# An attention layer and a non-local layer on one core: the first image's x kept whole, projections gathered in one gap, first-block differences made early, and one eviction per block moved to ScalarE

## The chip, the cores and the metric

The kernel runs on one core of one Trainium2 chip. The metric is device time in microseconds (us), from the first to the last instruction of the core and a little around it; lower is better. Engines are called PE (TensorE), DVE (VectorE), ACT (ScalarE), POOL (GpSimd) and SP (SyncE, which here only starts DMAs).

## What is computed

Two layers run one after the other on an image batch x of shape (2, 256, 64, 64), all in float32. With n = 64 * 64 = 4096 positions, 8 heads and d = 32:

```python
qkv = einsum('oc,bchw->bohw', w_qkv, x)                  # q, k, v
scores = einsum('bhdi,bhdj->bhij', q, k) / sqrt(d)       # 4096 x 4096 for each head
out = einsum('bhij,bhdj->bhdi', softmax(scores), v)
x = einsum('oc,bchw->bohw', w_proj, out) + x
# second layer: a non-local block with pooled keys, a 1x1 convolution, batch norm and a residual
```

The scores aren't stored: the kernel finds the maximum of every row of scores in a pass of its own, and uses it in a second pass over the same products.

## The kernel before, in words

A "quad" is four heads of one image; there are four quads, numbered n = 0 to 3, two for each image. A quad's attention is cut into eight blocks (i = 0 to 7) of 512 queries, and a block into 32 steps (j = 0 to 31) of 128 keys: 1024 steps in all. The order of the work is written out by hand, as generators that the main loop advances (`attend`, L551 to L591); each engine executes its own list of instructions in order. The list is nearly the order of the code; now and then the build moves a single instruction a little ahead. One such place matters here: `neg` of the next block (L380) stands ahead of DVE's add of step 26 (L473), though the code issues it after that add.

One step of block (n, i) holds, on PE: four score matmuls (`score`, L439, in two pairs, written into two PSUM tiles `s` that are kept over the whole block, each step adding the difference between its keys and those of the step before); four matmuls of the maxima pass of the *next* block (`product`, L286); and four matmuls of the step before that apply the weights to v (`weigh`, L463, tile `w`). ACT takes the exponential of both score tiles (L574, 128 x 1024 each). POOL adds up half of the exponentials for the softmax's denominator (L491, one 128 x 1024 add for each step), and starts an accumulating DMA for the other half in every second step (L497). DVE adds `w` to the running numerator `blk.num`, a slice of the result's tile y (L473).

The maxima pass of block (n, i + 1) runs through `maxes` while block (n, i) is worked on, two products in each half step, and is four steps ahead (`LEAD = 4`). Heads 0 and 1 take the plain way: DVE reduces each product of 512 keys (L298). Heads 2 and 3 take pairs of key chunks (`pair`, L300 to L308): the maximum of a and b is a + relu(b - a), so one product uses a difference of keys (`kd` or `last_kd`), ACT takes its relu into a tile `over` (L305), and DVE adds it to the second product and takes the maximum in one instruction (L312). A pair costs DVE one pass for 1024 keys where the plain way costs two. At the first block of quads 1 to 3 only the first half of the keys goes in pairs (L352), because `last_kd` still holds the differences of the quad before. Head 3 begins and ends each block with a plain product, so at the change of block, in step 27, DVE has one plain reduction more, and then the reduction `neg` (L380). POOL turns `neg` into three bf16 rows (L141 to L145), and PE and ACT into the tile `rows` (`make_rows`, L150 and L158, in step 30).

[...] four in the two score tiles, and four in the pool `ps_m` (`scratch`, L71), which gives its banks out in turn to the maxima products, to `w`, to the projections, to `rows` and to the denominator. A matmul into a bank waits until the bank's last reader is done.

The projections that make q, k and v for later blocks ("items", `make`, L168) are put between steps: `during` (L267) lists three for each block, and the loop issues them at j = 11, 19 and 27 (L588). For i below 6 they are q of the block after next, then k and v of the next quad; for i = 6 they are k, k, q, for i = 7 v, v, q. An item waits for its piece of x, loaded by SP into the only buffer of the pool `xs` (L171). For the last quad only the q items are left. `renew` (L250) has POOL make the key differences of the next quad at the end of block 7 and at the start of the next block.

A block's denominator is made in the next block: in its step 5 POOL makes `whole` (L510), in step 8 PE adds up the partitions (`den`, L518), and in step 27 POOL scales the numerator (L549).

Before the first block there is a start phase (L803 to L817): the items of quad 0, in the order k, q, k, v, q, v and then k, k, v, v, each cut in two halves with one group of four maxima products between halves.

Of the kernel before, what the change touches and what calls it, by code (L numbers as in the profile page):

```python
# [9 lines left out]
F32 = mybir.dt.float32  # L10
# [6 lines left out]
N = HH * WW  # L17
# [5 lines left out]
P = 128  # L23
NC = C // P
NB = 512
NI = N // NB
NJ = N // P
# [8 lines left out]
def conv_attention(  # L36
# [13 lines left out]
    nc = tc.nc  # L50
# [25 lines left out]
    def single(name):  # L76
        return probs.tile([P, 2, NB], F32, tag="one", name=name, bufs=ONES)
# [9 lines left out]
    def load_x(b, i, t):  # L87
        nc.sync.dma_start(
            out=t, in_=x[b].rearrange("(o p) n -> p o n", p=P)[:, :, bass.ts(i, NB)]
        )  # L90
        return t
# [76 lines left out]
    def make(what, n, i):  # L168
        b, qd = QUAD[n]
        if (b, i) not in held:  # L170
            name = f"x_{what}_{n}_{i}"  # L171
            if attending:
                held.clear()
                to = xs.tile([P, NC, NB], F32, tag="x", name=name)
            else:
                to = single(name)
            held[b, i] = load_x(b, i, to)
        xc = held[b, i]
        name = f"{what}_{b}_{qd}_{i}"
        pq = scratch(name)  # L180
        if what == "v":
            if i == 0:
                v[n] = qkv.tile([P, NJ, QH, D], F32, tag="v", name=f"v_{n}")
            for j in range(NB // P):
                for c in range(NC):
                    nc.tensor.matmul(  # L186
                        pq[:, bass.ts(j, P)],
                        xc[:, c, bass.ts(j, P)],
                        wv_sb[:, c, bass.ts(qd, P)],
                        start=(c == 0),  # L190
                        stop=(c == NC - 1),
                    )
                if j % 2 == 1:
                    yield
            nc.scalar.copy(v[n][:, bass.ts(i, NB // P)].rearrange("p j h d -> p (j h d)"), pq)
            return
        for c in range(NC):
            nc.tensor.matmul(  # L198
                pq,
                wqk_sb[:, c, qd, 0 if what == "q" else 1, :],  # L200
                xc[:, c, :],
                start=(c == 0),
                stop=(c == NC - 1),
            )
            yield
        if what == "q":
            to = q[n, i] = qkv.tile([P, NB], F32, tag="q", name=f"q_{n}_{i}", bufs=3)
        else:
            if i == 0:
                k[n] = qkv.tile([P, N], F32, tag="k", name=f"k_{n}")  # L210
            to = k[n][:, bass.ts(i, NB)]
        nc.scalar.copy(to, pq)
        if what == "k" and i % 2 == 0 and i > 0 and n == 0:
            between(n, i // 2 - 1)
        if what == "k" and i == NI - 1 and n == 0:
            rounds(n)
        if what == "k" and i % 2 == 1 and n == 0:
            if i == 1:
                kd[n] = qkv.tile([P, NI // 4, NB], F32, tag="kd", name=f"kd_{n}")
            differences(n, i // 2, (kd[n] if i < NI // 2 else last_kd)[:, i // 2 % (NI // 4), :])  # L220
        elif what == "k" and i == NI // 2 - 1:
            kd[n] = qkv.tile([P, NI // 4, NB], F32, tag="kd", name=f"kd_{n}")
            for c in range(2):
                differences(n, c, kd[n][:, c, :])
# [5 lines left out]
    def differences(n, c, to):  # L230
        two = k[n][:, bass.ts(c, 2 * NB)]
        nc.gpsimd.tensor_sub(to, two[:, NB:], two[:, :NB])  # L232
# [31 lines left out]

    def during(n, i):  # L267
        if i < NI - 2:
            return [("q", n, i + 2), ("k", n + 1, i), ("v", n + 1, i)]
        if i == NI - 2:  # L270
            return [("k", n + 1, i), ("k", n + 1, i + 1), ("q", n + 1, 0)]
        return [("v", n + 1, i - 1), ("v", n + 1, i), ("q", n + 1, 1)]


    reduced, cut = None, None
# [7 lines left out]
    def product(n, i, g, h, keys, ps=None):  # L283
        if ps is None:
            ps = scratch(f"ps_{n}_{i}_{g}_{h}")
        nc.tensor.matmul(  # L286
            ps,
            q[n, i][bass.ts(h, D), bass.ts(g, P)],
            keys[bass.ts(h, D), :],
            start=True,  # L290
            stop=True,
        )
        return ps
# [6 lines left out]
    def pair(n, i, g, h, jp):  # L300

        nonlocal cut
        ps = product(n, i, g, h, (kd[n] if jp < NI // 4 else last_kd)[:, jp % (NI // 4), :])
        over = work.tile([P, NB], F32, tag="over", name=f"over_{n}_{i}_{g}_{h}")
        cut = nc.scalar.activation(over, ps, AF.Relu)  # L305
        yield
        joint(product(n, i, g, h, k[n][:, bass.ts(2 * jp, NB)]), over, g, h, jp)
        yield  # L308
# [39 lines left out]
    def of_head(n, i, h):  # L348

        chunks = 0 if h < 2 else NI // 2 if i == 0 and n > 0 else NI  # L352
        pairs = [(g, jp) for jp in range(chunks // 2) for g in range(G)]
        plains = [(g, j) for g in range(G) for j in range(chunks, NI)]
        if h == 3:
            if not plains:
                g, jp = pairs.pop()
                plains = [(g, 2 * jp), (g, 2 * jp + 1)]
            plain(n, i, plains[0][0], h, plains[0][1])
            plains = plains[1:]  # L360
            yield
        for x in pairs:
            yield from pair(n, i, x[0], h, x[1])
        for x in plains:
            plain(n, i, x[0], h, x[1])
            yield

    def maxima(n, i):
        if (n, i) == (0, 0):
            yield from first_block()  # L370
        else:
            heads = [of_head(n, i, h) for h in range(QH)]
            for step in range(G * NI):

                for two in (0, 1), ((2, 3) if step % 2 == 0 else (3, 2)):
                    for h in two:
                        next(heads[h])
                    yield
        neg = work.tile([P, NB // P, QH], F32, tag="neg", name=f"neg_{n}_{i}")
        nc.vector.tensor_reduce(neg, part, AX.X, ALU.max, negate=True)  # L380
        rows.append(negate(f"{n}_{i}", neg))
        if i == 0 and n > 0:
            nc.vector.memset(part[:, :, 2:, :], LEAST)


    rows = []
# [8 lines left out]
    def advance(steps, n=1):  # L395
        for _ in range(n):
            next(steps, None)
# [3 lines left out]
    def make_rows():  # L401

        for i, r in enumerate(rows):
            if callable(r):
                if i in seen:
                    rows[i] = r()
                seen.add(i)


    def attend(b, y):  # L410
# [48 lines left out]
        def weigh(blk, j, p):  # L459

            w = scratch(f"w_{blk.name}_{j}")
            for h in range(QH):
                nc.tensor.matmul(  # L463
                    w[bass.ts(h, D), :],
                    v[blk.n][:, keys(j), h, :],
                    p[h // 2][:, h % 2, :],
                    start=True,
                    stop=True,
                )
            if j == 0:  # L470
                nc.vector.tensor_copy(blk.num, w)
            else:
                nc.vector.tensor_add(blk.num, blk.num, w)  # L473

# [77 lines left out]
        for qd in range(QUADS):  # L552
            for i in range(NI):
                blk = Block(qd, i)
                items = [x for x in during(blk.n, i) if x[1] < len(QUAD)]
                both = [None, None]
                for j in range(NJ):
                    if j % 2 == 0:
# [24 lines left out]
                    if j % 2 == 0:  # L583
                        make_rows()
                        if i > 0 and blk.n + 1 < len(QUAD) or i == 0 and blk.n > 0:
                            with tc.issue_after(added.ins) if added else ExitStack():
                                renew(i, j, blk.n)
                    elif j % 8 == 3 and j > 8 and items:  # L588
                        advance(make(*items.pop(0)), 9)
        weigh(*waiting)  # L590
        return normalize(blk)  # L591

# [204 lines left out]

    LEAD = 4
    AFTER = 8
    attending = False  # L800


    items = [("k", 0), ("q", 0), ("k", 1), ("v", 0), ("q", 1), ("v", 1)]  # L803
    for i in range(2, NI, 2):
        items += [("k", i), ("k", i + 1), ("v", i), ("v", i + 1)]
    for n, (what, i) in enumerate(items):
        pieces = make(what, 0, i)
        for piece in range(3):
            advance(pieces)
            if n > 3 and piece < 2:  # L810
                advance(maxes)
    advance(maxes, 4)
    advance(maxes)
    make_rows()
    advance(maxes, LEAD - 1)
    make_rows()
    advance(maxes, LEAD)  # L817
    held.clear()
    attending = True
    for b in range(B):  # L820
        y = big.tile([P, NC, N], F32, tag="y", name=f"y{b}")
        normal = attend(b, y)
# [57 lines left out]
```

## Time and profile before

| what | us |
|---|---|
| median of 3 runs | 3923.11 |
| the 3 runs | 3920.67 to 3923.43 |
| profiled execution, its own time | 3922.51 |
| its span, first to last instruction | 3920.7 |
| first weigh matmul of block (0, 0) | 105.98 |
| weigh matmuls of the first step, block (0, 2) to block (0, 3) | 308.82 to 410.68 |
| the same, block (3, 2) to block (3, 3) | 3054.85 to 3153.74 |

| engine | busy us | share of the span |
|---|---|---|
| PE | 3882.0 | 99% |
| DVE | 2940.4 | 75% |
| ACT | 2654.9 | 68% |
| POOL | 3051.9 | 78% |

A group line of the profile names the source line, the engine, the operation, the tile written and the tiles read, then shapes and count, then busy time in us, the mean in ns, and the idle time of the engine just before these instructions with what ended it. A line of the timeline has the start in us from the span's beginning, the length in us, the engine, the line, the operation and tiles, the count of instructions merged, and in brackets the idle time before. PE's matmuls are pipelined, so overlapping lengths are no contradiction, and its 99% isn't a measure of how well it is used: within a step PE often sits between the stages of a chain. A float32 matmul stands in the trace as two instructions.

### The profile page before, as it was taken

The numbers are of one execution on the slowest core, as the hardware profiler recorded it, in microseconds if no ns is written. First come the engines' busy times: TensorE is split into PE (matmuls) and PEld (weight loads), VectorE is DVE, ScalarE is ACT, GpSimd is POOL, SyncE is SP. The second block draws the span as 40 slices with busy tenths as digits, with TensorE's granted clock in tenths as the row PEclk, the third lists the DMA queues.
The fourth block names the chain that finished last, engine by engine and source line by source line (L and its number), as shares of the span: only waits on it lengthen the run. The fifth ranks groups of instructions, "written<-read, shape, count | busy, mean of one in ns | idle before, by whom it ended". The sixth has DMA issues, their size and how long they took to land.

```text
span 3920.7 us, 69957 instructions
## 1 busy us (share of the span) xinstructions
PE 3882.0 (99%) x27452; PEld 1370.0 (35%) x27452; DVE 2940.4 (75%) x5483; ACT 2654.9 (68%) x3296; POOL 3051.9 (78%) x1926
## 2 busy tenths in 40 slices
PE   8999999999999999999999999999999999999998
PEld 3333333333333333343333333333433333332333
DVE  5888888888888888874458888888888888885444
ACT  4777777777777777741137777777677787787011
POOL 1788888889888888871448889898899999997043
PEclk9999999999999999999999999999999999999999
DMA  1688888887888888880018888888888888889100
GB/s 57 139 168 169 167 170 168 174 169 167 166 167 169 165 169 169 172 195 6 22 38 167 167 173 170 170 171 175 165 173 169 169 170 168 167 167 188 54 16 27
DMA packets 113931, 569.40 MB, mean 145 GB/s; under 512 B 20296, under 2 KB 22600, under 8 KB 52416
## 3 DMA queue, kind: packets, MB, share of 16 engines
q0 software_dynamic: 68832, 501.25, 63.7%
q1 hardware_dynamic: 44080, 62.88, 4.6%
q8 instruction: 215, 3.52, 0.4%
q14 instruction: 116, 0.95, 0.1%
q10 hardware_dynamic: 688, 0.79, 0.1%
HBM read 54.78 MB, written 8.88 MB: 16 GB/s over the span
## 4 chain that ended last, share of the span: by engine, by line
PE 53%; DVE 2%; DMA 1%; ACT 0%; issue 0%; POOL 0%; DVEq 0%; ACTq 0%; POOLq 0%
PE s L439 14%; PE w L463 13%; PE ps L286 11%; PE y L736 6%; PE g L661 1%; DVE r L750 1%; PE f L704 1%; PE proj L604 1%; PE f L770 1%; PE q L198 1%; PE den L518 1%; PE tp L645 0%; PE tp L641 0%; PE v L186 0%; PE k L198 0%; DMA x_res<-in_x_dram 0%
## 5 line engine op out<-in xcount | busy, mean ns | idle before, releaser
L491 POOL TENSOR_TENSOR p<-p,p 128x1024 f32<-128x1024 f32 x945 | 2350.5, 2487 | 363.4 <-ACT p L574 338.4
L574 ACT ACTIVATE p<-s 128x1024 f32<-128x1024 f32 x2048 | 2085.9, 1023 | 593.3 <-PE ps L286 528.5
L286 PE MATMUL ps<-k,q 32*128 32x512 f32 x6232 | 2016.1, 627 | 4.0 <-DVE part L298 1.7
L298 DVE TENSOR_REDUCE part<-ps 128x1 f32<-128x512 f32 x2136 | 1369.0, 685 | 541.8 <-PE ps L286 541.6
L463 PE MATMUL w<-p,v 128*32 128x512 f32 x8192 | 1091.9, 605 | 0.6 <-ACT p L574 0.6
L439 PE MATMUL s<-q,mid_kd 32*128 32x512 f32 x3072 | 767.4, 615 | 0.0
L473 DVE TENSOR_TENSOR y<-y,w 128x512 f32<-128x512 f32 x992 | 679.1, 685 | 47.1 <-PE w L463 46.4
L312 DVE CUSTOM_DVE_ANT_0 ps<-ps,over 128x512 f32<-128x512 f32 x980 | 674.5, 691 | 34.3 <-PE ps L286 31.2
L286 PEld LDWEIGHTS ps<-k,q 32*128 32x128 f32 x6232 | 628.1, 183 | 43.3 <-DVE part L298 8.9
L305 ACT ACTIVATE over<-ps 128x512 f32<-128x512 f32 x916 | 541.9, 592 | 18.0 <-PE ps L286 12.6
L286 PE MATMUL ps<-kd,q 32*128 32x512 f32 x1056 | 517.0, 594 | 0.7 <-POOL kd L232 0.7
L439 PE MATMUL s<-q,kd 32*128 32x512 f32 x2048 | 512.2, 615 | 0.4 <-ACT p L574 0.3
L439 PE MATMUL s<-q,last_kd 32*128 32x512 f32 x2048 | 509.8, 614 | 0.7 <-ACT p L574 0.7
L463 PEld LDWEIGHTS w<-p,v 128*32 128x32 f32 x8192 | 161.1, 108 | 804.6 <-DVE part L298 775.0
L286 PE MATMUL ps<-last_kd,q 32*128 32x512 f32 x904 | 438.0, 593 | 2.4 <-POOL last_kd L232 2.4
L439 PEld LDWEIGHTS s<-q,mid_kd 32*128 32x128 f32 x3072 | 262.0, 183 | 413.9 <-ACT over L305 225.6
L497 POOL DMA_DIRECT2D p<-p x448 | 392.2, 875 | 4.4 <-issue 3.1
L439 PEld LDWEIGHTS s<-q,kd 32*128 32x128 f32 x2048 | 177.1, 183 | 295.4 <-ACT over L305 171.9
L439 PEld LDWEIGHTS s<-q,last_kd 32*128 32x128 f32 x2048 | 176.7, 183 | 275.8 <-ACT over L305 162.7
L736 PE MATMUL y<-p,kv 128*128 128x512 f32 x512 | 240.0, 608 | 6.4 <-DVE r L750 6.4
L785 ACT ACTIVATE p<-f 128x1024 f32<-128x1024 f32 x64 | 65.5, 1024 | 248.5 <-PE f L770 219.2
L732 POOL TENSOR_TENSOR sums<-sums,p 128x512 f32<-128x512 f32 x96 | 121.3, 1264 | 113.7 <-ACT p L785 109.9
(113 smaller groups left out, 2686.7 us busy)
## 6 DMA issues: line engine op xcount, KB each, us to landing
p<-p POOLq DMA_DIRECT2D x478, 1024.0 KB, 7.5
x_k<-in_x_dram SPq DMA_DIRECT2D x32, 512.0 KB
x_q<-in_x_dram SPq DMA_DIRECT2D x30, 512.0 KB
x_res<-in_x_dram SPq DMA_DIRECT2D x16, 512.0 KB
out_dram<-z SPq DMA_DIRECT2D x16, 512.0 KB
r<-flat SPq DMA_DIRECT2D x120, 64.0 KB
x_v<-in_x_dram SPq DMA_DIRECT2D x6, 512.0 KB
wqk_sb<-in_wqk_dram ACTq DMA_DIRECT2D x1, 512.0 KB
```

The costliest lines, as they stand in the source:

```text
L286: nc.tensor.matmul(ps, q[n, i][bass.ts(h, D), bass.ts(g, P)], keys[bass.ts(h, D), :], start=True, stop=True,)
L298: reduced = nc.vector.tensor_reduce(part[:, g, h, j : j + 1], ps, AX.X, ALU.max)
L305: cut = nc.scalar.activation(over, ps, AF.Relu)
L312: reduced = nc.vector.tensor_tensor_reduce(out=ps, in0=ps, in1=over, scale=1.0, scalar=LEAST, op0=ALU.add, op1=ALU.max, accum_out=part[:, ...
L439: nc.tensor.matmul(s[:, t, :], kj[bass.ts(h, D), :], q[blk.n, blk.i][bass.ts(h, D), :], start=False, stop=True, skip_group_check=j > 0,)
L463: nc.tensor.matmul(w[bass.ts(h, D), :], v[blk.n][:, keys(j), h, :], p[h // 2][:, h % 2, :], start=True, stop=True,)
L473: nc.vector.tensor_add(blk.num, blk.num, w)
L491: added = nc.gpsimd.tensor_add(blk.sums[0], blk.sums[0], p[0])
L497: sent = nc.gpsimd.dma_start(out=blk.sums[n], in_=two, accum_op=ALU.add)
L574: nc.scalar.activation(p[pair], s, AF.Exp, scale=scale)
L732: nc.gpsimd.tensor_add(acc[i][NC], acc[i][NC], p[:, j, :])
L736: nc.tensor.matmul(acc[i][o], wg[:, 2 * t + j, bass.ts(o, P)], p[:, j, :], **edge)
```

## The change

It has six parts.

1. The first image's x is loaded whole, by eight DMAs at the very start, into the space of the result's tile y (`x0`). The start phase no longer loads x into `single` buffers.
2. The start phase has a new order. k 0, k 1 and q 0 come first. Then come k 2 to k 7, v 0 and v 1, each an undivided item followed by four groups of maxima products; then q 1, and v 2 to v 7 with half a step of the next maxima pass before each.
3. Items. For i below 6, q stays at j = 11; k and v of the next quad share one load of x and come together at j = 30, in the gap in which `make_rows` also works. Block 6 holds five items (k and v at 11, q at 19, k and v at 30), block 7 one (q at 7). Blocks of the last quad have only their q item, as before.
4. `before_all`: at step 8 of block 7, POOL makes the last two differences of the next quad's keys into `first_kd`, in the buffer where x was. So heads 2 and 3 go in pairs over all keys in the first block of every quad, and the clearing of `part` (L383) goes away.
5. In step j = 26 of every block but the very last, `w` isn't added by DVE from PSUM: ACT copies it to a tile `t` in SBUF (a buffer of the tag `over`), and DVE adds `t` to `blk.num`. In the built program the ACT copy stands right after the exponential of step 27, and the DVE add stands where the old add stood, right behind `neg`.
6. Loop bookkeeping: `during` returns a dictionary by step.

```diff
@@ make
-            if attending:
-                held.clear()
-                to = xs.tile([P, NC, NB], F32, tag="x", name=name)
-            else:
-                to = single(name)
-            held[b, i] = load_x(b, i, to)
+            held.clear()
+            held[b, i] = load_x(b, i, xs.tile([P, NC, NB], F32, tag="x", name=name))
@@ during
+    first_kd = {}
+
     def during(n, i):
         if i < NI - 2:
-            return [("q", n, i + 2), ("k", n + 1, i), ("v", n + 1, i)]
+            return {11: [("q", n, i + 2)], NJ - 2: [("k", n + 1, i), ("v", n + 1, i)]}
         if i == NI - 2:
-            return [("k", n + 1, i), ("k", n + 1, i + 1), ("q", n + 1, 0)]
-        return [("v", n + 1, i - 1), ("v", n + 1, i), ("q", n + 1, 1)]
+            return {
+                11: [("k", n + 1, i), ("v", n + 1, i)],
+                19: [("q", n + 1, 0)],
+                NJ - 2: [("k", n + 1, i + 1), ("v", n + 1, i + 1)],
+            }
+        return {7: [("q", n + 1, 1)]}
+
+    def before_all(n):
+        held.clear()
+        first_kd[n] = xs.tile([P, NI // 4, NB], F32, tag="x", name=f"first_kd_{n}")
+        for c in range(2):
+            differences(n, NI // 4 + c, first_kd[n][:, c, :])
@@ pair
-        ps = product(n, i, g, h, (kd[n] if jp < NI // 4 else last_kd)[:, jp % (NI // 4), :])
+        those = kd[n] if jp < NI // 4 else first_kd[n] if i == 0 and n > 0 else last_kd
+        ps = product(n, i, g, h, those[:, jp % (NI // 4), :])
@@ of_head
-        chunks = 0 if h < 2 else NI // 2 if i == 0 and n > 0 else NI
+        chunks = 0 if h < 2 else NI
@@ maxima
-        if i == 0 and n > 0:
-            nc.vector.memset(part[:, :, 2:, :], LEAST)
@@ weigh
             if j == 0:
                 nc.vector.tensor_copy(blk.num, w)
+            elif j == NJ - LEAD - 2 and (blk.n, blk.i) != (len(QUAD) - 1, NI - 1):
+                t = work.tile([P, NB], F32, tag="over", name=f"w_{blk.name}")
+                nc.scalar.copy(t, w)
+                nc.vector.tensor_add(blk.num, blk.num, t)
             else:
                 nc.vector.tensor_add(blk.num, blk.num, w)
@@ attend
-                items = [x for x in during(blk.n, i) if x[1] < len(QUAD)]
+                items = during(blk.n, i)
...
-                    elif j % 8 == 3 and j > 8 and items:
-                        advance(make(*items.pop(0)), 9)
+                        if (i, j) == (NI - 1, 8) and blk.n + 1 < len(QUAD):
+                            with tc.issue_after(added.ins):
+                                before_all(blk.n + 1)
+                    for item in items.get(j, ()):
+                        if item[1] < len(QUAD):
+                            advance(make(*item), 9)
@@ the start phase
-    attending = False
-    items = [("k", 0), ("q", 0), ("k", 1), ("v", 0), ("q", 1), ("v", 1)]
-    for i in range(2, NI, 2):
-        items += [("k", i), ("k", i + 1), ("v", i), ("v", i + 1)]
-    for n, (what, i) in enumerate(items):
-        pieces = make(what, 0, i)
-        for piece in range(3):
-            advance(pieces)
-            if n > 3 and piece < 2:
-                advance(maxes)
-    advance(maxes, 4)
-    advance(maxes)
-    make_rows()
-    advance(maxes, LEAD - 1)
-    make_rows()
-    advance(maxes, LEAD)
+    x0 = big.tile([P, NC, N], F32, tag="y", name="x0")
+    for i in range(NI):
+        held[0, i] = load_x(0, i, x0[:, :, bass.ts(i, NB)])
+    for what, i in (("k", 0), ("k", 1), ("q", 0)):
+        advance(make(what, 0, i), 3)
+    for what, i in [("k", i) for i in range(2, NI)] + [("v", 0), ("v", 1)]:
+        advance(make(what, 0, i), 3)
+        advance(maxes, G)
+    advance(make("q", 0, 1), 3)
+    for i in range(2, NI):
+        advance(maxes)
+        advance(make("v", 0, i), 3)
+        if i in (3, 5):
+            make_rows()
+    advance(maxes, 2 * LEAD - NI + 2)
```

More of the change, by code (lines that the diff above doesn't have):

```diff
@@ L799, in conv_attention @@
     AFTER = 8
-    attending = False
-    items = [("k", 0), ("q", 0), ("k", 1), ("v", 0), ("q", 1), ("v", 1)]
-    for i in range(2, NI, 2):
-        items += [("k", i), ("k", i + 1), ("v", i), ("v", i + 1)]
-    for n, (what, i) in enumerate(items):
-        pieces = make(what, 0, i)
-        for piece in range(3):
-            advance(pieces)
-            if n > 3 and piece < 2:
-                advance(maxes)
-    advance(maxes, 4)
-    advance(maxes)
-    make_rows()
-    advance(maxes, LEAD - 1)
-    make_rows()
-    advance(maxes, LEAD)
+    x0 = big.tile([P, NC, N], F32, tag="y", name="x0")
[13 more added lines that the diff above has]
+    advance(maxes, 2 * LEAD - NI + 2)
     held.clear()
-    attending = True
     for b in range(B):
```

## The prediction

> **What bounds the kernel now.** I read the engines' shares first, then the chain of waits, then the timeline of one step and of the change of block.
>
> ```profile
> PE 3882.0 (99%) x27452; PEld 1370.0 (35%) x27452; DVE 2940.4 (75%) x5483; ACT 2654.9 (68%) x3296; POOL 3051.9 (78%) x1926
> ...
> L491 POOL TENSOR_TENSOR p<-p,p 128x1024 f32<-128x1024 f32 x945 | 2350.5, 2487 | 363.4 <-ACT p L574 338.4
> ...
> L473 DVE TENSOR_TENSOR y<-y,w 128x512 f32<-128x512 f32 x992 | 679.1, 685 | 47.1 <-PE w L463 46.4
> ```
>
> PE is the bound, but 99% overstates it: in a step its three groups stream 6 x 0.43 = 2.56 us, and a step lasts 2.96 us. The rest is a closed chain: w, then score and maxima products, then DVE's reduction of the first product, whose bank the next w needs. POOL's adds fill 2.49 us of a step, its DMA starts more: it is nearly always busy. The chain prices what lies between steps:
>
> ```profile
> 2066.70 1.92 PE q L198 x4
> ...
> 2117.87 1.98 PE v L186 x16
> ...
> 2168.55 1.91 PE q L198 x4
> ...
> 2888.57 1.91 PE q L198 x4
> 2987.46 1.91 PE q L198 x4
> ```
>
> q to q, a block with three items lasts 101.85 us, one of the last quad with only q 98.89. So k and v together cost 2.96 there, though k is 1.91 and v 1.98: about 0.94 of v is free. The timeline of block (3, 2) shows why:
>
> ```profile
> 3131.59 1.06 PE L463 MATMUL w<-p,v 128*32 128x512 f32 x8
> ...
> 3133.80 1.89 DVE L298 TENSOR_REDUCE part<-ps 128x1 f32<-128x512 f32 x3 [0.39 <-PE ps L286]
> 3134.55 1.06 PE L463 MATMUL w<-p,v 128*32 128x512 f32 x8
> ...
> 3135.61 0.69 DVE L312 CUSTOM_DVE_ANT_0 ps<-ps,over 128x512 f32<-128x512 f32 x1
> ...
> 3135.70 0.84 POOL L497 DMA_DIRECT2D p<-p  x1
> ...
> 3136.30 2.62 POOL L491 TENSOR_TENSOR p<-p,p 128x1024 f32<-128x1024 f32 x1
> ...
> 3136.46 0.29 DVE L380 TENSOR_REDUCE neg<-part 128x16 f32<-128x128 f32 x1
> ...
> 3136.66 0.68 DVE L473 TENSOR_TENSOR y<-y,w 128x512 f32<-128x512 f32 x1
> ...
> 3137.26 1.99 DVE L298 TENSOR_REDUCE part<-ps 128x1 f32<-128x512 f32 x3
> ...
> 3137.40 1.12 PE L286 MATMUL ps<-k,q 32*128 32x512 f32 x2
> ...
> 3138.45 1.06 PE L463 MATMUL w<-p,v 128*32 128x512 f32 x8
> ```
>
> w to w is 2.96 us, then 3.90 at the change of block. DVE has three reductions in a row, the joint pass, neg, and only then the add of w. A product waits for that add's bank until 3137.40, and w 26's successor comes 0.94 late. With a v item at this place, DVE's extra work lies beside PE's. Note POOL: its add is in flight from 3136.30 to 3138.92, over DVE's add.
>
> [...] (1) [...] Today's add reads w in PSUM, one SBUF input; the new one reads `blk.num` and `t`, two. The trace holds a case with two, L489 in the last block:
>
> ```profile
> L489 DVE TENSOR_TENSOR p<-p,p x15: 1218/1226/4104, 3551.1 to 3625.5; 128x1024 f32<-128x1024 f32 x15
> ```
>
> (count, then shortest/median/longest ns), and from the timeline there:
>
> ```profile
> 3556.53 2.00 DVE L489 TENSOR_TENSOR p<-p,p 128x1024 f32<-128x1024 f32 x1
> ...
> 3560.70 2.36 POOL L491 TENSOR_TENSOR p<-p,p 128x1024 f32<-128x1024 f32 x1
> ...
> 3562.59 1.56 DVE L489 TENSOR_TENSOR p<-p,p 128x1024 f32<-128x1024 f32 x1
> ```
>
> Alone it takes 1.22. At 3562.59 POOL's add still had 0.47 to run: it took 1.56, 0.34 more. At 3556.53, 0.91 left: 0.78 more. At 3551.11 it took 4.10, with POOL's add behind a DMA start at its side. So DVE waits for POOL's add to end, less 0.14. (2) [...] So what stands behind the held add waits too; the trace agrees, nothing starts behind L489 until it is done. [...]
>
> **The change, part by part.** Sums are against the profiled execution (3922.51, span 3920.7), 0.6 below the median of 3923.11.
>
> *Step 26 through ACT.* ACT is idle then (no relu in step 27), so its copy of 0.59 hides, and the bank comes free early: PE's wait at 3137.40 goes. What is late next is DVE. Its add is ready at 3136.66, behind neg as now; POOL's add has begun 0.36 earlier and holds until 3138.92. By (1) DVE waits to 3138.78, adds in 0.60 (the spacing of back-to-back passes), and the reduction that now starts at 3137.26 starts at 3139.38. It takes 0.69, and 0.06 later w 27 starts: 3140.13, in place of 3138.45. The change of block then costs 5.58 - 2.96 = 2.62 over a plain step, not 0.94. Queued behind the held add are the two reductions, the next plain one and the add of w 27; w 27 waits for the first. Bounds of the unknown stall: 0 (DVE first; then DVE's row of passes alone makes the step 3.48, an excess of 0.52) to 2.9 (as at 3551.11). I take 2.12, because the offset of 0.30 to 0.38 stands in 25 of the 31 changes of block that I compared, blocks without a k or v item among them.
>
> *Items, i below 6, quads 0 to 2: 18 blocks.* Now: k 1.92, v 1.98 with the change of block hidden in it, rows 0.34 (w to w at step 30): 4.24. Then: rows, k and v in one gap: 0.34 + 1.92 + 1.98 less one 0.2 turn-round of PE (between two projections it streams on: 1.71 for k) = 4.02. With 2.62 bare, 6.64: +2.40 each, **+43.2**. The item queue in SP: one load fewer, each with 13 to 19 steps of 2.96 us of cover; if that cover failed, a load's 7 us would show.
>
> *Blocks 6 and 7 of quads 0 to 2.* Now 102.49 + 106.58 (w to w): block 7 has DVE reductions beyond what a step holds (3.4 in every second step, +3.9 in all), and q items used in the very next step (+0.6 each). Then: 32 x 2.96 = 94.6, den 0.87, block start 0.17. Block 6: + 3.70 (k, v) + 1.92 (q) + 2.62 + 4.02 = 107.9. Block 7: + 1.92 + 2.62 + 0.34 = 100.5. Sum 208.4, -0.7 each, **-2**. Pairs cost ACT 16 more relus of 0.59 in a block, as in every other block: hidden. POOL's two `first_kd` passes (1.3 each) fill its spare 0.15 a step up to step 26; POOL's backlog in the next block, which now costs block (3, 0) some 1.5 us at `den`, would grow by 2 without the stall, but the stall gives POOL 2 back: **+1** (0 to +4).
>
> *Last quad, i = 0 to 5.* No items move; 2.62 for 0.94: +1.68 x 6 = **+10**. In (3, 6) no maxima pass follows, DVE has room: 0.
>
> *Start.* k 0, k 1, q 0 end at 13.5 (as k, q, k do now). Then eight times an item and two pairs. The joint passes between 80.4 and 89.3, without items, show 2.9 us a pair; with two half items now 4.26, so 1.4 of 1.8 is not hidden: 2 x 2.9 + 1.4 = 7.2, x 8 = 57.6, ending at 71.1. q 1 with its copy 2.6, six times half a step and v 3.0, rows and two half steps 1.5: 93.2, against 99.28 now for the first row subtraction, and half a us less to the first w: **-6.6** (-17 with items hidden, -1 with nothing hidden). The eight loads are issued at once and the last has 20 us.
>
> Sum: -6.6 + 43.2 - 2 + 1 + 10 = +45.6: 3968.1, on the median's scale 3968.7, some 3969.
>
> **The rivals.**
>
> [...] The margin is 0.36 us by start, less if POOL's add really begins when its DMA start ends (3136.54). If POOL waits 0.6 instead, the excess is 0.52: 2.1 less at 30 changes of block, -63, and POOL's backlog +3: 3909. For it: POOL did wait at 3580.97 (3.13 for 2.36), where DVE had begun 0.32 before. Against: at 3551.11 DVE lost though it had begun 0.36 before POOL. It decides from the point where DVE's add starts before POOL's.
>
> *The clock drops as well.* PE stands still from 3137.54 to 3140.13, 2.6 us. [...] Here matmuls took 1.06 to 1.22 instead of 0.59 from 92 to 102, after a gap of 1.69 us; after one of 1.98 (L604's wait for y) they did not. At half clock 2.56 of PE work takes 5.12; [...] half of the 30 cases +21, all +43: 3990 to 4012.
>
> *A short stall*, about a third of 2.1 with the start at its best: 3920, no change.
>
> **Chances.** 0.2% (7.8 us) is about what a measurement of this kernel can tell from no change. Stall as computed 0.48; with the clock 0.23; DVE first 0.24; short stall 0.05. Slower 0.71, same 0.05, faster 0.24. The forecast is the likeliest, 3969; its own range, from start and stall bounds, is 3950 to 3992. The range that holds 8 in 10 reaches into both rivals: 3906 to 4003.
>
> **What would show it.** In the profile after: DVE's add that reads `over` at 2.7 to 2.8 us mean (about 0.69 if DVE is first, with POOL adds of 3.1 beside it); w 26 to w 27 at 5.6 (3.5); k to v spaced 1.7 in the gap of step 30, and about 4.0 + 2.96 there; block 7 with no steps of 3.4; first w near 99. The forecast is wrong if the new add is short.

## The result, and the profile after

The changed kernel takes 4047.54 us (median of 5 runs, 4046.62 to 4050.64); the kernel before, run beside it, 3923.11. The ratio is 1.0322 with a 95% interval of 1.031 to 1.0334: slower, by 124 us. The prediction was 3969, with a range up to 4003: the sign was right, the size was not. The profiled execution took 4046.81, its span is 4045.0.

The engines' shares and three groups of the profile after:

```profile
PE 3916.0 (97%) x27452; PEld 1374.0 (34%) x27452; DVE 3003.2 (74%) x5480; ACT 2695.8 (67%) x3372; POOL 3070.0 (76%) x1932
...
L504 POOL TENSOR_TENSOR p<-p,p 128x1024 f32<-128x1024 f32 x945 | 2346.8, 2483 | 367.5 <-ACT p L587 355.7
...
L470 PE MATMUL w<-p,v 128*32 128x512 f32 x8192 | 1112.9, 616 | 91.5 <-DVE part L307 90.8
...
L486 DVE TENSOR_TENSOR y<-y,w 128x512 f32<-128x512 f32 x961 | 658.3, 685 | 75.3 <-PE w L470 74.2
```

PE is busy 34 us longer with the same 27452 matmuls, so some of them ran slower. POOL's adds (2487 ns before) and DVE's plain add of w (685) are what they were. But w, before which PE stood idle for 0.6 us in all, now waits 91 us for DVE's reduction of the first product, the step that closes the chain. The line before the change:

```profile
L463 PE MATMUL w<-p,v 128*32 128x512 f32 x8192 | 1091.9, 605 | 0.6 <-ACT p L574 0.6
```

The instructions of the new add's line (count, then shortest, median and longest in ns):

```profile
L484 DVE TENSOR_TENSOR y<-y,w x31: 681/4022/4103, 187.6 to 3654.9; 128x512 f32<-128x512 f32 x31
```

4.02 us in the median, where I had 2.72 (2.12 of wait and 0.60). The timeline of block (3, 2), the same place as shown before, shows what it waits for:

```profile
3238.43 1.07 PE L470 MATMUL w<-p,v 128*32 128x512 f32 x8
...
3239.57 0.58 ACT L483 COPY w<-w 128x512 f32<-128x512 f32 x1
...
3240.16 2.63 POOL L504 TENSOR_TENSOR p<-p,p 128x1024 f32<-128x1024 f32 x1
...
3240.55 4.02 DVE L484 TENSOR_TENSOR y<-y,w 128x512 f32<-128x512 f32 x1
...
3242.47 1.54 POOL L562 TENSOR_TENSOR y<-y,r 128x512 f32<-128x512 f32 x1
3243.67 0.99 POOL L141 CAST terms<-neg 128x16 bf16<-128x16 f32 x1
3244.49 1.87 DVE L307 TENSOR_REDUCE part<-ps 128x1 f32<-128x512 f32 x3
...
3245.22 1.66 PE L470 MATMUL w<-p,v 128*32 128x512 f32 x8 [3.62 <-DVE part L307]
```

The copy on ACT is in time, and `neg` is too. DVE's add starts 0.39 after POOL's add, as foreseen. But POOL has a second operation right behind: L562, the scaling of the numerator of the block before. DVE's add ends at 3244.57, 0.56 after that multiplication, not after the add of step 27. The reductions stand behind it, and w 27 (the weigh matmuls of step 27) starts 6.79 us after w 26, where the block before the change had 3.90. Then the clock of PE, which the trace records as the granted share of full speed: four stretches of 3.4 us from 3239.4 (columns: stretch, its length, busy time and instructions of PE, weight load, DVE, ACT and POOL, then the granted clock, the DMA share and GB/s):

```profile
3239.40:3242.80 3.40, 2.21 (x20) 1.29 (x16) 3.29 (x5) 2.89 (x5) 3.40 (x4) 1.00 0.69 142
3242.80:3246.20 3.40, 0.98 (x8) 0.16 (x8) 3.40 (x4) 0.40 (x1) 3.11 (x7) 0.91 0.93 193
3246.20:3249.60 3.40, 3.40 (x20) 1.21 (x16) 1.47 (x4) 0.66 (x1) 1.96 (x1) 0.59 0.00 0
3249.60:3253.00 3.40, 3.40 (x32) 1.07 (x32) 3.01 (x7) 2.90 (x5) 2.26 (x2) 1.00 0.50 101
```

PE stands nearly still in the second stretch (0.98 us busy of 3.40), and in the third it works at about half clock (0.59) for as much time with fewer matmuls. The step after the long one takes 4.56 us here, and 5.5 to 5.6 in 12 blocks, instead of 2.96. The chain of waits shows the pieces of quad 2:

```profile
2300.75 1.77 PE k L194 x4
2302.52 1.78 PE v L182 x16
2343.80 1.91 PE q L194 x4
...
2450.78 1.91 PE q L194 x4
```

k and v are now back to back, 1.77 and 1.78. From q to q a block lasts 106.98, where it was 101.85.

Taking every start of w from both traces and subtracting, step by step, the difference falls into few places. All steps 26 together take 40 us more, the two steps after them 52 more, the steps 29 and 30, where k and v now lie, 75 more, and steps 0 to 25, which the items have left, 43 less. The start takes 0.8 more. (A 2.2 more in block (3, 7) and the stretch behind the last w, which is shorter by about as much, cancel.)

### The profile page after: what moved, and what is told of

Read it like the earlier page. It is cut to its first block, busy times and chain, and to the rows that moved or that the text cites. A ratio compares the mean times of both kernels' runs of the same rounds, so it can differ in the third digit from the quotient of the medians.

```text
span 4045.0 us, 70025 instructions
## 1 busy us (share of the span) xinstructions
PE 3916.0 (97%) x27452; PEld 1374.0 (34%) x27452; DVE 3003.2 (74%) x5480; ACT 2695.8 (67%) x3372; POOL 3070.0 (76%) x1932
## 4 chain that ended last, share of the span: by engine, by line
PE 49%; DVE 3%; issue 2%; DMA 1%; POOL 0%; ACT 0%; DVEq 0%; POOLq 0%; ACTq 0%
PE s L446 13%; PE w L470 12%; PE ps L295 10%; PE y L753 5%; PE proj L621 1%; PE g L678 1%; DVE r L767 1%; PE f L721 1%; PE f L787 1%; DVE part L307 1%; DMA p<-p 1%; PE q L194 1%; PE den L531 0%; PE tp L662 0%; PE tp L658 0%
## 5 line engine op out<-in xcount | busy, mean ns | idle before, releaser
L295 PE MATMUL ps<-k,q 32*128 32x512 f32 x6142 | 2043.3, 635 | 5.4 <-DVE part L322 3.4
L307 DVE TENSOR_REDUCE part<-ps 128x1 f32<-128x512 f32 x2046 | 1315.2, 685 | 583.9 <-PE ps L295 583.9
L470 PE MATMUL w<-p,v 128*32 128x512 f32 x8192 | 1112.9, 616 | 91.5 <-DVE part L307 90.8
L322 DVE CUSTOM_DVE_ANT_0 ps<-ps,over 128x512 f32<-128x512 f32 x1025 | 706.6, 692 | 35.1 <-PE ps L295 25.0
L486 DVE TENSOR_TENSOR y<-y,w 128x512 f32<-128x512 f32 x961 | 658.3, 685 | 75.3 <-PE w L470 74.2
L315 ACT ACTIVATE over<-ps 128x512 f32<-128x512 f32 x961 | 569.3, 592 | 18.6 <-PE s L446 9.7
L446 PE MATMUL s<-q,last_kd 32*128 32x512 f32 x2048 | 542.1, 650 | 4.0 <-ACT p L587 4.0
L295 PE MATMUL ps<-kd,q 32*128 32x512 f32 x1056 | 533.4, 605 | 0.0
L446 PEld LDWEIGHTS s<-q,mid_kd 32*128 32x128 f32 x3072 | 270.2, 183 | 442.2 <-ACT over L315 257.5
```

Source lines behind the costliest of these rows:

```text
L295: nc.tensor.matmul(ps, q[n, i][bass.ts(h, D), bass.ts(g, P)], keys[bass.ts(h, D), :], start=True, stop=True,)
L307: reduced = nc.vector.tensor_reduce(part[:, g, h, j : j + 1], ps, AX.X, ALU.max)
L322: reduced = nc.vector.tensor_tensor_reduce(out=ps, in0=ps, in1=over, scale=1.0, scalar=LEAST, op0=ALU.add, op1=ALU.max, accum_out=part[:, ...
L446: nc.tensor.matmul(s[:, t, :], kj[bass.ts(h, D), :], q[blk.n, blk.i][bass.ts(h, D), :], start=False, stop=True, skip_group_check=j > 0,)
L470: nc.tensor.matmul(w[bass.ts(h, D), :], v[blk.n][:, keys(j), h, :], p[h // 2][:, h % 2, :], start=True, stop=True,)
```

## The experiments

Nine kernels were run; each ratio is to the kernel before on the same chip.

**1. The copy taken back, all else as changed.**

```diff
-            elif j == NJ - LEAD - 2 and (blk.n, blk.i) != (len(QUAD) - 1, NI - 1):
-                t = work.tile([P, NB], F32, tag="over", name=f"w_{blk.name}")
-                nc.scalar.copy(t, w)
-                nc.vector.tensor_add(blk.num, blk.num, t)
```

> The changed kernel with only the copy through ScalarE taken back: DVE adds w from PSUM in step 26 as before. Theory 1 [...]: w 26 to w 27 falls from 6.80 to 3.90 us in the blocks without an item there, the next step from 4.6 or 5.6 to 2.96, no half-clock intervals after the start; the gap of step 30 stays at 6.84. 27 blocks x (2.9 + 2.1) = 135 us less than 4047.5: 3912, range 3905 to 3930. Rival A (the loss is in the items that were gathered in one gap, which leaves the change of block bare): the copy matters little, 4000 or more. Rival B (POOL's backlog and the start): between, 4030 or more, with the stalls of 5 us in blocks (1, 0) and (3, 0) unchanged.

Measured: 3925.27, ratio 1.0011 (1.0002 to 1.002). w 26 to w 27 is 3.90 in nearly all blocks, the next step 2.96, the gap of step 30 stays at 6.84. So the four lines of the copy, with the add's wait and the half clock after it, hold almost the whole loss. Against this kernel the changed one loses 69.4 us in step 26 and 52.4 in the two steps after it, 121.8 of 123.2 us of span. Rivals A and B fall. All other parts of the change together come to +1.1 us of span (+2.9 by the medians).

**2. The copy alone, put into the kernel before.** The same four lines, added.

> The kernel before with nothing but the copy through ScalarE in step 26 (items, start and differences as before). Theory 1: the add waits for POOL here too, w 27 is 3.84 us late; in quads 0 to 2 the item in step 27 (1.98 us of PE) runs inside that wait, so w 26 to w 27 is about 6.8 where it was 4.94 (+1.86 x 24 = +45), and PE stands still under 2 us, so no half clock. In the last quad, without an item, 6.8 for 3.90 and a half clock after it (+2.9 + 2.1, x 6 = +30). Sum 3998, range 3965 to 4010. Rival A (the items' places are the loss, the copy alone is harmless): 3910 to 3925, w 26 to w 27 at 4.94 or below. Rival C (the half clock comes from the add and not from PE's standing still): half-clock intervals in quads 0 to 2 too, 4050.

Measured: 3994.14, ratio 1.0182 (1.0167 to 1.0197). w 26 to w 27 is 6.80 in 17 of the 24 blocks with an item in it (it was 4.94, or 5.57 in block 6) and 6.79 in the six of the last quad without one (3.90). The item of 1.98 us lies inside the wait and costs nothing. In the last quad a half-clock step of 4.56 or 5.59 follows each time; in the first three quads it follows in 3 of the 22 blocks with a longer step 26. So the add needs no help from the other parts to do its harm, and the half clock came with the longer standing still of PE: 3.78 us in the last quad, where it followed each time, for 1.98 in most blocks with an item.

**3. POOL's multiplication moved from step 27 to step 29.**

```diff
-                for _ in range(13):
+                for _ in range(15):
                     yield
             with tc.issue_after(added.ins):
                 nc.gpsimd.tensor_mul(blk.num, blk.num, r)
```

> The changed kernel with POOL's scaling of the numerator of the block before moved from step 27 to step 29, so that nothing but the add of step 27 is queued on POOL while DVE's new add waits. Theory 1 ([...] the queued multiplication of 1.22 us was what my sum of 2.12 us lacked): the new add takes 2.9 us (ready to end) and w 26 to w 27 is 5.58 in all blocks, as the two blocks without that multiplication have it; 27 x 1.22 = 33 less if the half clock stays (block (2, 0) had it after 5.59): 4014; up to 55 more less if it goes: 3960. Rival D ([...] the late end has another reason, such as the DMA start or neg): w 26 to w 27 stays at 6.80, the time at 4047.

Measured: 4006.95, ratio 1.0216 (1.0201 to 1.0231). The line of the add, and the change of block in the last quad:

```profile
L484 DVE TENSOR_TENSOR y<-y,w x31: 680/2811/2889, 188.7 to 3613.3; 128x512 f32<-128x512 f32 x31
```

```profile
3308.01 2.64 POOL L504 TENSOR_TENSOR p<-p,p 128x1024 f32<-128x1024 f32 x1
3308.19 0.29 DVE L389 TENSOR_REDUCE neg<-part 128x16 f32<-128x128 f32 x1
3308.39 2.82 DVE L484 TENSOR_TENSOR y<-y,w 128x512 f32<-128x512 f32 x1
3310.30 1.01 POOL L141 CAST terms<-neg 128x16 bf16<-128x16 f32 x1
```

Now the add ends 0.56 after POOL's add, and w 26 to w 27 is 5.58 in all 25 blocks that stall, the figure of my prediction to the hundredth. Rival D falls. The half clock stays: 23 of the 25 are followed by a step of about 4.57.

**4. k in step 19 and v in step 27 again, with the copy.**

```diff
-            return {11: [("q", n, i + 2)], NJ - 2: [("k", n + 1, i), ("v", n + 1, i)]}
+            return {11: [("q", n, i + 2)], 19: [("k", n + 1, i)], 27: [("v", n + 1, i)]}
```

> The changed kernel, copy and all, with the items of the blocks i below 6 back in their old places (k in step 19, v in step 27, one load of x for both); blocks 6 and 7, start and differences as changed. Theory 1: v runs inside the stall, w 26 to w 27 stays at about 6.8 with v in it; PE stands still under 2 us, so no half clock in these 18 blocks; the gap of step 30 falls from 6.84 to 3.29, k costs 1.92 in step 19. Per block -3.55 + 1.92 - 2.1 = -3.7, x 18 = -67: 3980, range 3965 to 3995. If the half clock stays in these blocks although PE stands still for less than 2 us: 4018. If v isn't hidden in the stall (its bank or ACT's eviction behind it): +36, 4016, with w 26 to w 27 at 8.8.

Measured: 3990.25, ratio 1.0175 (1.016 to 1.019), 57 less than as changed. w 26 to w 27 stays at 6.80 with v inside it; of the 15 blocks that have v in a long wait, one is followed by a half-clock step. This shows again what experiment 2 showed: filled with 2 us of work, the wait is followed by half clock in few blocks.

**5. The same items, without the copy.** Experiments 1 and 4 joined.

> The changed kernel without the copy, and with k in step 19 and v in step 27 again for blocks i below 6; blocks 6 and 7, start and differences as changed. What is left is parts 1, 2 and 4 and the items of blocks 6 and 7. Theory 1 (gathering the items in one gap costs 0.62 a block, because v then no longer covers the change of block): 18 x 0.62 = 11 less than without the copy alone: 3914, range 3911 to 3918, so about 8 less than before, from block 7 (98.9 where it was 106.6) less block 6 (106.2 where it was 102.5), less 4.7 of POOL's stalls in block (1, 0). Rival (the gap costs nothing): 3923 to 3925.

Measured: 3915.95, ratio 0.9984 (0.9978 to 0.9991). Blocks of i below 6 take 101.91 instead of 102.48 in experiment 1: v was covering the change of block, and gathering k and v in one gap gives back less than that. The rival falls.

**6. The new start alone, in the kernel before.** Parts 1 and 2 of the change, nothing else.

> The kernel before with only the start changed: x of the first image whole in the result's place, k 0, k 1, q 0 first, then an undivided item and four groups of maxima products in turn. My prediction gave this part -6.6 us (-17 to -1). The changed kernel's trace shows 8.11 us for an item with its four groups where I had 7.2, and the first weigh matmul at 106.73 against 105.98. Theory 1 (the part is what it looks like in the changed kernel, whatever follows): first weigh matmul near 106.7, the rest as before: +0.7, 3923, range 3921 to 3926. Rival (the start is slowed by something else in the changed kernel, and gains by itself): first weigh matmul at 99 to 101, 3917.

Measured: 3921.44, ratio 0.9998 (0.999 to 1.0006): no difference that can be measured. The first weigh matmul stands at 107.15 (105.98 before). The stretch of one item and four groups in the changed kernel shows why; columns as above:

```profile
21.45:29.56 8.11, 7.68 (x38) 3.06 (x36) 5.62 (x17) 4.71 (x9) 1.26 (x1) 1.00 0.00 0
```

It repeats every 8.11 us, and PE is busy 7.68 of them. The four groups take 6.19 (23.37 to 29.56), the item 1.92, and nothing of the item is hidden.

**7. As 5, with the old start.**

> As the one with v in step 27 and no copy, and with the start of the kernel before. If the new start costs 0.7 to 0.8: 3913, range 3910 to 3917, the fastest of all by these terms. If POOL's stalls of 5 us in block (1, 0) come with the differences made early and not with the start, they are here too.

Measured: 3914.00, ratio 0.998 (0.9972 to 0.9988). Its interval overlaps that of experiment 5: the start costs 1 to 2 us, if anything (the first w stands at 106.63 there, at 105.58 here). POOL's stalls are there: block (1, 0) takes 106.15, its neighbours 101.91, and with the new start alone (experiment 6) it took 101.98. They come from the differences made early, or from the shorter block 7, and not from the start.

**8. POOL without work while DVE's add is due**, copy and all else as changed. POOL's add of step 27 stands behind that of step 28, and the multiplication in step 29.

```diff
+            elif j == NJ - 5:
+                blk.held = p
             elif j < NJ - 1:
                 added = nc.gpsimd.tensor_add(blk.sums[0], blk.sums[0], p[0])
@@ the loop over j
                     add(blk, j, p, two)
+                    if j == NJ - 4 and blk.held is not None:
+                        added = nc.gpsimd.tensor_add(blk.sums[0], blk.sums[0], blk.held[0])
@@ normalize
-                for _ in range(13):
+                for _ in range(15):
```

> The changed kernel, copy and all, but POOL has nothing to run while DVE's new add is due: the add of step 27 stands behind that of step 28, and the scaling of the numerator is in step 29. Theory 1 (the add is held by POOL's operation, not by its own two SBUF inputs): the new add takes 0.6 to 0.7 us in most blocks, w 26 to w 27 is 3.45 to 3.5 (it was 3.45 in the two blocks where DVE came first), no half clock; 27 x 0.42 = 11 below the kernel without the copy: 3914. Against that POOL loses up to 2.5 us a block that it has to catch up with 0.15 of room a step; if that shows as stalls, 3914 to 3990, with w 26 to w 27 at 3.45 all the same. Rival E (an add with two SBUF inputs is slow beside anything, or the ACT copy comes late): the add stays over 2 us and w 26 to w 27 at 5 or more.

Measured: 3914.49, ratio 0.9982 (0.9976 to 0.9989), 133 us faster than the changed kernel, by nothing but the order of POOL's list. The add's line, and its place in block (3, 3):

```profile
L485 DVE TENSOR_TENSOR y<-y,w x31: 679/681/1405, 188.3 to 3522.8; 128x512 f32<-128x512 f32 x31
```

```profile
3228.09 0.88 POOL L513 DMA_DIRECT2D p<-p  x1
...
3229.09 0.68 DVE L485 TENSOR_TENSOR y<-y,w 128x512 f32<-128x512 f32 x1
...
3230.43 1.06 PE L471 MATMUL w<-p,v 128*32 128x512 f32 x8 [0.28 <-DVE part L307]
```

0.68 us with the same two SBUF inputs; w 26 to w 27 is 3.45, and there is no half clock. The 2.5 us that POOL loses in each block don't show: block (3, 3) takes 98.51, less than the 98.90 before. Rival E falls. This is what the copy could have been worth: 0.45 for a change of block.

**9. What was found, put together:** the old start, items as in 5, and the copy with POOL's order as in 8.

> What the runs found, put together: the start of the kernel before, k in step 19 and v in step 27 for blocks i below 6, the differences made early and the items of blocks 6 and 7 as changed, the copy through ScalarE with POOL free of work while DVE's add is due (its add of step 27 behind that of step 28, the scaling in step 29). Theory 1: 3.45 instead of 3.90 at w 26 in the 9 to 11 blocks without an item there, nothing in the others, where the item covers the change of block (4.94 stays): 3914.0 - 10 x 0.45 = 3909.5, range 3906 to 3914; 13 below the kernel before. If POOL can't catch up in the blocks that are 102 us or shorter: 3914 to 3925.

Measured: 3909.09, ratio 0.9967 (0.9955 to 0.9979): 13 us faster than the kernel before. The gain is in blocks 6 and 7, and 0.45 in each of nine changes of block that no item covers; those of block 7 gain or lose up to 0.3. It came out at the sum of its parts.

## Why the prediction was wrong, point by point

The sum of the prediction beside what the starts of w show. "Other parts" is experiment 1 less the kernel before, "copy" is the changed kernel less experiment 1:

| term | predicted | other parts | copy | together |
|---|---|---|---|---|
| start | -6.6 | +0.7 | +0.1 | +0.8 |
| 18 blocks, i < 6, quads 0 to 2 | +43.2 | +14.2 | +78.1 | +92.3 |
| blocks 6 and 7, with the layer between | -2 | -12.8 | +11.1 | -1.7 |
| last quad, i = 0 to 6 | +10 | +0.8 | +32.3 | +33.2 |
| block (3, 7) | 0 | +0.4 | +1.8 | +2.2 |
| POOL's backlog | +1 | in the rows above | | |

The sum says +45.6 and the spans +124.3, so it missed by 78.7. Of this 52.4 is the clock, which the sum left out; 19.0 is the stall in step 26 (69.4 measured, 30 times 1.68 in the sum); 7.4 is the start. What is left cancels.

**The steps that failed** are the length of the stall and the clock. The stall: "POOL's add has begun 0.36 earlier and holds until 3138.92. By (1) DVE waits to 3138.78." The direction held: DVE's add waits for POOL (4.02 us in the median, 0.68 in experiment 8, where POOL's two operations stand later), and the reductions and w 27 wait behind it. The term was too small, because I ended POOL's hold at the add of step 27 and left out the multiplication that is queued behind it in the same step (L549 before, L562 after). I had named it in the description, and the kernel before has it in the block that I read, 0.30 before the recorded end of POOL's add:

```profile
3138.62 1.52 POOL L549 TENSOR_TENSOR y<-y,r 128x512 f32<-128x512 f32 x1
```

With it the wait is 3.3 us, not 2.1, and the excess of the step 3.84, not 2.62; experiment 3 takes the multiplication away and gives the predicted 5.58. In 23 blocks the excess was 3.84, in 2 blocks, which have no numerator of a block before to scale, 2.62. In 5 blocks the add took 0.68 to 1.42: there POOL's list ran late, and its add of step 27 hadn't begun. The kernel before has POOL late in the same five (DVE's add of step 26 starts 2.5 to 3.9 us after the last start of an add on POOL, elsewhere 0.30 to 0.38), and the sum counted the stall in them too. My upper bound for the stall, 2.9, came from an add in the last block that waited for one POOL operation, so it was too low for two.

**The clock** is the larger part of the miss. It was a rival of its own with a chance of 0.23, and should have been a part of the forecast: a stand-still of 2.57 us, which my stall already implied, was followed by half clock in 23 of 25 blocks of experiment 3. Its price for a block, which I had estimated at 1.4 (43 us for 30 blocks), is 1.6, or 2.6 to 2.9 where two intervals of 3.41 us follow. Together 52.4 us. With the longer stall it came after 24 of the 25 blocks that stalled, so even the rival's upper end, 4012, was too low.

**The items**, without the stall: I had 0.94 + 4.02 - 4.24 = 0.72 a block, the trace of experiment 1 has 102.48 - 101.86 = 0.62. Right, though the gap of step 30 is 6.84 - 2.96 = 3.88 in the trace, for my 4.02, whose own terms (0.34 + 1.92 + 1.98 less 0.2) add up to 4.04. Blocks 6 and 7 without the stall: 106.2 and 98.9 measured, 106.2 (107.9 less 1.68) and 98.8 (100.5 less 1.68) from the working. Right. With the copy, block 7 lost or gained no more than 0.5 in any of the three quads, for POOL ran late there. That the row as a whole, -1.7, stands so near the predicted -2 is luck: the working had six stalls of 1.68 in it, and the trace has two, which with the half clock cost 5.5 and 5.6.

**POOL's backlog**, put at +1 (0 to +4), is 5.3: block (1, 0) loses 4.8 beyond the items' 0.6, (3, 0) 0.5. The POOL groups in block (0, 7), first before, then in experiment 1, and what PE waits for at the start of block (1, 0) there:

```profile
L491 POOL TENSOR_TENSOR p<-p,p 128x1024 f32<-128x1024 f32 x30 | 74.1, 2470 | 12.5 <-ACT p L574 12.1
```

```profile
L498 POOL TENSOR_TENSOR p<-p,p 128x1024 f32<-128x1024 f32 x30 | 75.2, 2506 | 5.9 <-ACT p L581 5.1
```

```profile
PE s L446 <- ACT p L581: 2.6, 2, 1.5
```

POOL had 12.5 us of room ahead of its adds in block 7, and has 5.9. I counted the two new passes, 2.5 us, but not that the block became 7.7 us shorter: time saved on PE is room lost on POOL. ACT, whose exponentials PE waits for, waited for POOL's work in turn: in the first 34 us of block (1, 0) it stood 5.0 us for the accumulating DMAs that POOL starts and 2.3 for `whole`, where the kernel before has 0.7 for `whole` in the same stretch. How much of the stall each of the two makes wasn't tried.

**The start** failed by itself, hidden in the sum: 8 x (8.11 - 7.2) = +7.3 of the 7.4 that it was off. I took 2.9 for a pair from a stretch without items, and 0.4 of the item as hidden; a pair takes 3.1 beside an item, and nothing is hidden. Even my bound for "nothing hidden", -1, was too good.

What isn't settled: block (3, 7), into which no copy goes, is about 2 us longer in every kernel with the copy (83.8 to 85.3 for 81.6 to 82.2). The excess stands in its steps 5 and 6 (4.62 and 3.49 as changed, 4.16 and 2.25 in experiment 1); its cause is open.

## What to carry to other kernels

When an operation begins to read both its inputs from SBUF on DVE, look at POOL's whole list from that moment on, not only at the operation in flight; here 0.68 us with w in PSUM became 4.02 with both in SBUF, and moving two POOL instructions brought it back to 0.68. If a stall makes PE stand still for as long as it did here (1.98 us was followed by half clock in 3 of 30 cases, 2.57 in 23 of 25 blocks of experiment 3, 3.78 in 23 of 23), price what the clock does afterwards with it, and ask which work could lie inside: 2 us of projections in the gap took most of the half clock away. A move that frees one engine can shorten the room of the others (POOL's went from 12.5 us to 5.9 in block (0, 7)): check what POOL or DVE catches up in the block that gets shorter.

## What the runs showed of the hardware

- **Which of DVE and POOL waits.** With w in PSUM, DVE's add took 0.68 us beside POOL's add in flight (3136.66 in block (3, 2) before, POOL's from 3136.30 to 3138.92). With both inputs in SBUF, as changed, and begun 0.31 to 0.39 after POOL's add, it took 4.02 to 4.10 in 24 blocks and 2.89 in the two without the multiplication; begun 0.46 before POOL's add (block (1, 6)), it took 0.68. The recorded starts don't decide it throughout: in blocks (0, 7) and (2, 7) of experiment 2 DVE's add begins 0.24 before POOL's and takes 4.64 and 4.65 all the same, and so waits the add at 3551.11 below, begun 0.36 before POOL's. What I had not expected: a waiting DVE add didn't always run between two operations that are queued on POOL. With the 128x512 multiplication behind the add it ended 0.56 after the multiplication (24 of 24 times as changed). With a cast of 128x16 behind the add (experiment 3), or a DMA start behind a difference of keys (blocks (0, 7), (1, 7) and (2, 7) as changed), it ended 0.55 to 0.56 after the one operation, and the cast of experiment 3 took 0.99 in the median, for 0.51 before the change. The kernel before has one more case, in the last block:

```profile
3551.11 4.10 DVE L489 TENSOR_TENSOR p<-p,p 128x1024 f32<-128x1024 f32 x1
3551.47 5.97 POOL L491 TENSOR_TENSOR p<-p,p 128x1024 f32<-128x1024 f32 x2
```

The first of the two POOL adds ends at 3554.13, and DVE's add, 1.22 alone, ends at 3555.21: it was done before the second, which starts 0.08 after the end of the first and takes 3.24 (2.49 in the mean). So two inputs or a larger size of the operation behind weren't enough here to keep DVE waiting. Nor was an early start: the multiplication starts 0.32 before the recorded end of the add, and the cast of experiment 3 does so by 0.34. Whether the two together decide wasn't tried.

- **The clock goes by a grid.** The record of the granted clock holds 1.0 and 0.5. In the traces of both kernels its half-clock intervals begin whole multiples of 3.413 us apart (as changed at 296.44, 402.25 and 511.48, the later two 31 and 63 times 3.413 after the first; before at 71.50 and 91.98, 6 times), and behind a change of block they last one or two times 3.413. Below, PE counts as still from 0.43 us after the start of its last matmul to the next start, for score matmuls that follow on each other start 0.43 to 0.44 apart (3239.96, 3240.40 and 3240.83 in block (3, 2) as changed). 2.33 to 2.58 us inside one interval of the grid was followed by half clock (23 times in experiment 3); 2.57 us split over two intervals as 1.97 and 0.59, 1.24 and 1.33, or 2.03 and 0.54 was not. 1.98 us was in 3 of 30 cases (experiments 2 and 4), and shorter ones were at times: 1.62 us in block (1, 7) of experiment 2. So the length of one stand-still isn't all that counts; what else does is open. 3.78 us, in the changed kernel, was in all 23 blocks, for one interval (next step 4.5 to 4.6) or for two (5.5 to 5.6).
